# Small columns spread through DRAM instead of by TensorE, in a four-layer graph kernel whose instruction order is computed from assumed costs

**The chip, the cores and the metric.** One core of a Trainium2 chip. The time is the device time of one execution in microseconds (us), the median of the runs of a kernel.

## The reference, cut to what matters

The input is `x`, 128 graphs of 64 nodes with 512 features, and `adj`, a 64 x 64 matrix for each graph. Four layers follow, each of them `x = x + layer(relu(layernorm(x)))`. The change touches three of them:

```python
# layer 1
s = (x @ w) @ a                                   # one score for each node
A = tanh((s[:, :, None] + s[:, None, :]) / 8) * 8
A = exp(leaky_relu(A, 0.1)) * adj
A = A / sum(A, -1) * sum(adj, -1)                 # the normaliser, one number for each row
out = A @ x @ w
# layer 2
weight = adj * exp(query @ key.T)
out = (weight / sum(weight, -1)) @ value
# layer 3
e = leaky_relu(sj[:, None, :] + si[:, :, None] + ab, 0.2)
trans = adj * exp(e); trans = trans / sum(trans, -1)
H = sum over k = 0, 1, 2 of (trans^k @ x) @ Wk[k] + bk[k]
```

All is float32.

## The kernel before

Sixteen groups of 8 graphs (512 nodes, 4 tiles of 128 nodes, two graphs in a tile) go first through layers 0 and 1, then, in a second half, through layers 2 and 3. The large products are Strassen products, so TensorE does seven block products for eight.

A node's score is a column: one number on each partition. For `s[i] + s[j]` each partition also needs the 64 scores of its graph along its free dimension. The kernel before does this with TensorE: it multiplies the column into a diagonal and multiplies that by a block of ones.

```python
def bcast_sum(col, row, r, extra=None):
    dg, p, z = Buf("dg"), Buf("ps"), Buf("ee")
    dve(0.42, lambda: nc.vector.tensor_mul(dg.t, ident2[:, None, :].to_broadcast([P, T, C]),
                                           row()[:, :, None].to_broadcast([P, T, C])), r, [dg])
    pe(c_mm(256, 1), lambda: nc.tensor.matmul(p.t[:, :T * C], ones_bd, dg.t.rearrange("p t c -> p (t c)"),
                                              start=True, stop=True), [dg], [p])
    # ... (layer 3 adds a constant to col)
    dve(0.42, lambda: nc.vector.tensor_add(z.t, p.t[:, :T * C].rearrange("p (t c) -> p t c", t=T),
                                           col()[:, :, None].to_broadcast([P, T, C])), [p, *r], [z])
    return z
# layer 1, normaliser: column sums by ones_bd, twice, and a reciprocal of 256 columns
    pe(c_mm(256, 2), sums, [z, ad], [pd])
    dve(2.0, lambda: nc.vector.reciprocal(rn.t, half(0)), [pd], [rn])
# layer 2: sums of the weights by eight passes of one column
    pd, rd = col_sums(PT, PTk), Buf("col")
    # ... four products of 512 columns, each scaled by rd and added to x
# layer 3
    dot(lambda h=h: h.t, lambda s=s: c3_b[:, s, :], lambda t=t, s=s: ss.t[:, t, s:s + 1], ...)
    z = bcast_sum(lambda: ss.t[:, :, 1], lambda: ss.t[:, :, 0], ssk, extra=kap)
```

`pe(cost, fn, reads, writes)` and its likes (`dve`, `act`, `pool`, `dma`) do not emit an instruction. They put an operation into a graph, with an assumed cost and the current priority `G.prio`. At the end `Graph.run` plays the whole program with these costs. At each step it takes the operation that can start first and, among equals, the one of the lowest priority number, and it emits the instructions in that order. On the chip every engine then keeps to its list.

```python
LATENCY = {"PE": 0.30, "DVE": 0.12, "ACT": 0.12, "POOL": 0.15, "SP": 2.0}
# ... in run(), after an operation o has been placed at time t:
end = t + o.cost + self.LATENCY[o.eng]
for q in o.succ:
    q.ready = max(q.ready, end if q.eng != o.eng else t + o.cost)
# ... the priorities
STRETCH, PERIOD1, PERIOD2, LEAD = (1.65, 1.86, 2.69, 2.67), 80.0, 75.8, 1.5
for g in range(NG):
    G.prio = (g - LEAD) * PERIOD1
    # load of group g ...
    G.prio = g * PERIOD1        # then layers 0 and 1; inside a layer, step(us) adds us * STRETCH[layer]
```

Note the line with `q.ready`. A successor on another engine waits for the latency, a successor on the same engine does not. All transfers are issued by SP (the engine SyncE), so a transfer that reads what another transfer wrote is taken to be ready as soon as the first one has been issued.

## Time and profile before

| | before |
|---|---|
| time, median of 3 runs | 2470.34 us |
| span of the profile (of an execution of 2473.58 us) | 2471.6 us |
| TensorE busy / not busy | 2416.3 us / 55.3 us |
| mean granted TensorE clock | 0.99 |
| period of one group, first half / second half | 73.84 / 74.18 us |

A period is the time from a point of one group to the same point of the next; sixteen periods make a half. "Not busy" is the span less the busy time.

### The profile page before, as it was taken

Reading aid. Unit: us, or ns where it says so; the run is one execution under the profiler, and the core shown is the slowest. Engines: PE = TensorE matmul, PEld = TensorE weight load, DVE = VectorE, ACT = ScalarE, POOL = GpSimd, SP = SyncE. Lnnn points to the kernel's source line nnn. Section 1 sums busy time; section 2 is a strip of 40 time slices with the busy share of each in tenths; the row PEclk is TensorE's granted clock in tenths of the full one; section 3 lists DMA queues with packets and bytes.
Section 4 is the critical chain, followed back from the end, with each engine's and each line's share of the span. In section 5 each row is a group of like instructions: output and inputs, shape, how many; then the busy total and the mean of one; then the engine's idle time right before and its main releaser. Section 6 shows DMA issues by size and latency. Waiting matters only on the chain.

```text
span 2471.6 us, 32994 instructions
## 1 busy us (share of the span) xinstructions
PE 2416.3 (98%) x12058; PEld 1878.4 (76%) x12058; DVE 1808.8 (73%) x4128; ACT 1176.1 (48%) x1626; POOL 723.9 (29%) x842
## 2 busy tenths in 40 slices
PE   8999999999999999999989999999999999999998
PEld 4566767776677776677777888888888888888886
DVE  8678888888888888888875566665566665566663
ACT  4355554655554555454633445343445343445321
POOL 3223344333444333444221212221212221212220
PEclk9989999999999999999999999999999999999998
DMA  5242222222222222222431233212223222222211
GB/s 187 68 103 52 60 59 66 73 56 49 63 64 61 73 56 52 60 69 56 120 111 46 58 69 69 69 43 61 55 69 73 61 48 60 56 69 67 58 22 34
DMA packets 323698, 163.39 MB, mean 66 GB/s; under 512 B 278096, under 2 KB 278096, under 8 KB 323536
## 3 DMA queue, kind: packets, MB, share of 16 engines
q1 hardware_dynamic: 323536, 161.28, 26.3%
q8 instruction: 95, 1.56, 0.3%
q14 instruction: 67, 0.55, 0.1%
HBM read 59.52 MB, written 34.60 MB: 38 GB/s over the span
## 4 chain that ended last, share of the span: by engine, by line
PE 86%; DVE 9%; ACT 2%; DMA 1%; issue 1%; POOL 0%; DVEq 0%; ACTq 0%; POOLq 0%
PE ps L570 56%; PE ps L779 15%; PE ps L509 3%; PE ps L883 2%; PE ps L834 2%; PE ps L697 2%; DVE s_s_vu_tt L562 2%; PE ps L804 2%; DVE rT_a L562 1%; DVE u L588 1%; PE ps L607 1%; DVE ee L722 1%; PE ps L869 1%; DVE z_hT L590 1%; ACT rT_a L520 1%
## 5 line engine op out<-in xcount | busy, mean ns | idle before, releaser
L570 PE MATMUL ps<-wb_mem,rT_a 128*128 128x256 f32 x2056 | 480.7, 382 | 8.1 <-ACT rT_a L520 4.5
L492 POOL TENSOR_TENSOR rs<-ve,mhalf 128x1 f32<-128x1 f32 x320 | 202.2, 634 | 919.9 <-DVE ve L491 841.3
L570 PEld LDWEIGHTS ps<-wb_mem,rT_a 128*128 128x128 f32 x2056 | 389.5, 191 | 80.6 <-issue 13.8
L500 ACT ACTIVATE h<-x,nm,rs 128x512 f32<-128x512 f32 x256 | 208.0, 815 | 319.0 <-DVE nm L499 309.0
L570 PE MATMUL ps<-wb_mem,s_s_vu_tt 128*128 128x256 f32 x1152 | 274.3, 381 | 1.2 <-DVE x L737 0.9
L570 PE MATMUL ps<-wb_mem,tmp_mB_s 128*128 128x256 f32 x1152 | 263.1, 380 | 0.0
L570 PEld LDWEIGHTS ps<-wb_mem,s_s_vu_tt 128*128 128x128 f32 x1152 | 219.0, 191 | 48.3 <-issue 14.4
L570 PE MATMUL ps<-wb_mem,mT_a 128*128 128x256 f32 x1016 | 246.8, 382 | 5.7 <-DVE y_qT L600 5.0
L570 PE MATMUL ps<-wa_mem,mT_a 128*128 128x512 f32 x512 | 244.5, 602 | 2.8 <-ACT mT_a L511 1.5
L570 PEld LDWEIGHTS ps<-wb_mem,tmp_mB_s 128*128 128x128 f32 x1152 | 217.8, 190 | 37.0 <-issue 7.2
L570 PEld LDWEIGHTS ps<-wb_mem,mT_a 128*128 128x128 f32 x1016 | 188.7, 190 | 48.5 <-DVE y_qT L600 13.2
L538 ACT COPY u<-ps 128x256 f32<-128x256 f32 (+1 forms) x160 | 73.1, 457 | 277.7 <-PE ps L570 227.1
L570 PE MATMUL ps<-wa_mem,s_s_vu_tt 128*128 128x512 f32 x384 | 181.0, 595 | 1.5 <-DVE z_hT L590 1.0
L489 DVE BATCH_NORM_STATS2 st<-x 128x6 f32<-128x512 f32 x256 | 175.1, 684 | 3.6 <-DMA x<-xm 3.0
L570 PEld LDWEIGHTS ps<-wa_mem,mT_a 128*128 128x128 f32 x512 | 94.7, 192 | 95.5 <-issue 85.6
L896 POOL TENSOR_TENSOR u<-u,bk_b 128x256 f32<-128x256 f32 x96 | 79.1, 823 | 300.9 <-DVE u L542 177.8
L540 DVE TENSOR_TENSOR u<-ps,u 128x256 f32<-128x256 f32 (+1 forms) x160 | 84.5, 528 | 104.4 <-PE ps L570 44.3
L520 ACT COPY rT_a<-z_hT 128x1024 uint16<-128x1024 uint16 x128 | 145.9, 1160 | 15.5 <-DMA z_hT<-tmp_mB_s 15.4
L509 PEld LDWEIGHTS ps<-bd,h 128*128 128x128 f32 x1024 | 129.5, 195 | 24.1 <-issue 10.8
L518 ACT COPY o<-h 128x1024 uint16<-128x1024 uint16 x128 | 133.3, 1041 | 22.9 <-DVE o L358 21.3
L677 ACT ACTIVATE z_hT<-z_hT 128x512 f32<-128x512 f32 x128 | 80.5, 630 | 127.5 <-DVE z_hT L590 124.0
L666 POOL TENSOR_TENSOR x<-x,h 128x512 f32<-128x512 f32 x64 | 91.1, 1423 | 169.2 <-ACT h L500 168.9
(181 smaller groups left out, 4242.6 us busy)
## 6 DMA issues: line engine op xcount, KB each, us to landing
x<-in_x_dram SPq DMA_DIRECT2D x64, 256.0 KB, 2.7
xm<-x SPq DMA_DIRECT2D x64, 256.0 KB, 2.0
x<-xm SPq DMA_DIRECT2D x64, 256.0 KB, 2.8
out_dram<-x SPq DMA_DIRECT2D x64, 256.0 KB, 2.0
adj<-in_adj_dram SPq DMA_DIRECT2D x32, 256.0 KB, 2.9
wb_mem<-in_Wk_dram SPq DMA_DIRECT2D x6, 512.0 KB, 6.6
wa_mem<-in_W1T_dram SPq DMA_DIRECT2D x2, 1024.0 KB, 8.5
wb_mem<-in_W2T_dram SPq DMA_DIRECT2D x4, 512.0 KB, 6.2
```

Of the source, the lines that this page charges most:

```text
L489: dve(0.69, lambda i=i: nc.vector.bn_stats(st.t[:, i, :], src(i)), [r[i]], [(st, i)])
L492: pool(0.57, lambda: nc.gpsimd.tensor_tensor(rs.t, ve.t, mhalf, ALU.pow), [ve], [rs])
L500: act(0.82, lambda: nc.scalar.activation(h.t, xx.t, AF.Relu, bias=nm.t, scale=rs.t), [xx, nm, rs], [h])
L509: nc.tensor.matmul(quad(p)[:, c, :], h.t[:, c * P:(c + 1) * P], rhs(), start=True, stop=True)
L518: act(1.05, lambda: nc.scalar.copy(u16(planes.t).rearrange("p (q c) -> p q c", q=2), u16(src()).rearrange("p (c q) -> p q c", q=2)), ksrc, ...
L520: act(1.16, lambda: nc.scalar.copy(u16(dst()).rearrange("p c (k q) -> p c k q", q=2), u16(back()).rearrange("p (q c r) -> p c r q", q=2, c ...
L540: dve(c_v(n), lambda: nc.vector.tensor_add(at(1)(), p2.t[:, :n], at(0)()), [p2, (U, 0)], [(U, 1)])
L570: nc.tensor.matmul(p.t[:, :n], lhs()[:, c, :], rhs(c), start=first and c == 0, stop=c == kc - 1, skip_group_check=True)
L666: pool(1.3, lambda xx=xx, h=h: nc.gpsimd.tensor_add(xx.t, xx.t, h.t), [h, xx], [xx])
L677: act(0.63, lambda: nc.scalar.activation(z.t[:, cols], z.t[:, cols], AF.Relu), [(z, j)], [(z, j)])
L779: nc.tensor.matmul(pair(p.t)[:, o, :], a, b, start=first and o == 0 and c == 0, stop=c == 1, skip_group_check=True)
L896: pool(0.75, lambda: nc.gpsimd.tensor_add(U.t[:, iv], U.t[:, u[1]], add()), [u, ka], [v])
```

## The change

The intent is to take small work off TensorE, the bound engine, and to thin out the edges. It has five parts: (1) a column is stored to DRAM (`row`) and loaded back onto all 64 partitions of its graph (`rw`), for layer 1's and layer 3's scores and for layer 1's normaliser, which is now summed along the free dimension; (2) layer 2's `v` gets a column of ones, so its product brings the sums along; (3) layer 2's weight product moves to the start; (4) the loads of the setup and of W3 are placed anew; (5) the numbers of the priorities are new, with the preludes of layers 1 and 3 (the chain of small steps before the large products) drawn forward by 10.2 and 24.2 us.

```diff
+    def across(col, r):
+        b = Buf("rw")
+        d = dram.tile([P, T], F32, name=f"row{len(rows)}")
+        key = ("row", len(rows))
+        rows.append(d)
+        dma(4, lambda: nc.sync.dma_start(d, col()), r, [key])
+        def back():
+            for s in HALVES:
+                nc.sync.dma_start(b.t[s].rearrange("p c t -> p (c t)"),
+                                  d[s].rearrange("c t -> (c t)").partition_broadcast(C))
+        dma(128, back, [key], [b])
+        return b
     def bcast_sum(col, row, r, extra=None):
-        # diagonal product, matmul by ones_bd, sum out of PSUM
+        b, z = across(row, r), Buf("ee")
+        # ...
+        dve(0.42, lambda: nc.vector.tensor_add(z.t, by_node(b), col()[:, :, None].to_broadcast([P, T, C])), [b, *r], [z])
@@ layer 1, normaliser @@
-        pe(c_mm(256, 2), sums, [z, ad], [pd])
-        dve(2.0, lambda: nc.vector.reciprocal(rn.t, half(0)), [pd], [rn])
+        # num, den: two sums along the free dimension, then den = num / den (4 columns)
+        rn = across(lambda: den.t, [den])
@@ layer 2 @@
-        pd, rd = col_sums(PT, PTk), Buf("col")
+        # v is [P, 2, D + 1]; two products for each tile, of 257 and 256 columns; one reciprocal for each tile
@@ layer 3 @@
+        G.prio -= KNOBS[1]                      # layer 1 likewise with KNOBS[0]
@@ costs and priorities @@
-        return G.op("SP", kb / 190.0, fn, r, w)
+        return G.op("SP", kb / 350.0, fn, r, w)
-    STRETCH, PERIOD1, PERIOD2, LEAD = (1.65, 1.86, 2.69, 2.67), 80.0, 75.8, 1.5
+    STRETCH, PERIOD1, PERIOD2, LEAD = (1.72, 2.82, 2.69, 2.68), 81.0, 75.5, 0.88
+    KNOBS = (10.2, 24.2, 45.0, 88.7, 160.0, -976.9, -988.0, -973.4, -974.0, 5.0, -970.0, -939.5,)
# ... cut: setup_l2 at the start, W3's loads, rows for gamma and beta, the loop of layer 3's setup
```

More of the change, by code (lines that the diff above doesn't have):

```diff
@@ L181, in tile_adj_preln_d4 @@
         "u5": ([P, 3, D], 2), "u2": ([P, 3, D // 2], 1),
-        "bd": ([P, T, P], 4), "dg": ([P, T, C], 1), "ee": ([P, T, C], 2),
+        "bd": ([P, T, P], 4), "rw": ([P, C, T], 1), "ee": ([P, T, C], 2),
         "st": ([P, 2, 6], 6), "mv": ([P, 2], 10), "ve": ([P, 1], 10), "rs": ([P, 1], 10), "nm": ([P, 1], 10),
@@ L190, in tile_adj_preln_d4 @@
         ([("rT", [P, KH, P], 3)], [("a3", [P, 3 * KD, P], 2)]),
-        ([("s2", [P, 3, 4, P], 1), ("s1", [P, 3, 2, P], 2)], [("vu", [P, 2, D], 2), ("tt", [P, T, 2, P], 1)]),
+        ([("s2", [P, 3, 4, P], 1), ("s1", [P, 3, 2, P], 2)], [("vu", [P, 2, D + 1], 2), ("tt", [P, T, 2, P], 1)]),
         ([("y", [P, D], 2)], [("qT", [P, 2, 2 * P], 2)]),
@@ L264, in dma @@
     def dma(kb, fn, r, w):
-        return G.op("SP", kb / 190.0, fn, r, w)
+        return G.op("SP", kb / 350.0, fn, r, w)
     def quad(b):
         return b.t.rearrange("p (c k) -> p c k", c=4)
+    STRETCH, PERIOD1, PERIOD2, LEAD = (1.72, 2.82, 2.69, 2.68), 81.0, 75.5, 0.88
+    KNOBS = (10.2, 24.2, 45.0, 88.7, 160.0, -976.9, -988.0, -973.4, -974.0, 5.0, -970.0, -939.5,)
+    HEAD = KNOBS[5:]
     ident = const.tile([P, P], F32, name="ident")
     make_identity(nc, ident)
-    ident2 = const.tile([P, C], F32, name="ident2")
-    nc.vector.tensor_add(ident2, ident[:, :C], ident[:, C:])
     ones = const.tile([P, P], F32, name="ones")
     nc.vector.memset(ones, 1.0)
-    ones_bd = const.tile([P, P], F32, name="ones_bd")
-    nc.vector.memset(ones_bd, 0.0)
-    for s in HALVES:
-        nc.vector.memset(ones_bd[s, s], 1.0)
     mhalf = const.tile([P, 1], F32, name="mhalf")
@@ L313, in temp, with load_group @@
         return load_tmp("tmp", D, lambda t: t, src)
-    xt, adjs, xmid = {}, {}, {}
-    def load_group(g, src):
+    xt, adjs, xmid, rows = {}, {}, {}, []
+    def load_group(g, src, apart=0.0):
         b = Buf("adj")
@@ L323, in load_group @@
             at, key = src(g, t)
+            G.prio += apart
             dma(256, lambda xx=xx, at=at: nc.sync.dma_start(xx.t, at), key, [xx])
@@ L334, in tile_adj_preln_d4 @@
     G.prio = -1000.0
-    load_group(0, x_in)
+    bq_c = load_cols("bq_c", bq, KD)
+    load_group(0, x_in, HEAD[4])
+    G.prio = HEAD[5]
     load_w("w1", w1_sb, W1T)
     b1_b = [load_row(b1[i * D:(i + 1) * D]) for i in range(2)]
-    gb2 = const.tile([P, KH, 2], F32, name="gb2")
-    dma(8, lambda: nc.sync.dma_start(gb2[:, :, 0], gamma), [], ["gb2g"])
-    dma(8, lambda: nc.sync.dma_start(gb2[:, :, 1], beta), [], ["gb2b"])
+    G.prio = HEAD[6]
+    gb2 = const.tile([P, 2, KH], F32, name="gb2")
+    dma(8, lambda: nc.sync.dma_start(gb2[:, 0, :], gamma), [], ["gb2g"])
+    dma(8, lambda: nc.sync.dma_start(gb2[:, 1, :], beta), [], ["gb2b"])
     load_w("w2", w2_sb, W2T)
@@ L344, in tile_adj_preln_d4 @@
     load_w("w", w_sb, w)
-    bq_c = load_cols("bq_c", bq, KD)
     wa_b = Buf("row")
@@ L359, in dot, with combine @@
                                                          accum_out=acc()), r, [*w, j])
-    def combine(name, w_, x_, kc, n, eng):
+    def combine(name, w_, x_, kc, n, eng, olds=()):
         k2 = [w_[:, :kc, :], w_[:, kc:, :]]
@@ L369, in combine @@
         T1 = name + "T1"
-        G.op(eng, cost, lambda: sub(x_[:, 1], blk(1, 1), blk(0, 1)), [*low, *high], [(name, "x1")])
-        G.op(eng, cost, lambda: sub(blk(0, 1), blk(0, 1), blk(0, 0)), [*low, (name, "x1")], [T1])
+        G.op(eng, cost, lambda: sub(x_[:, 1], blk(1, 1), blk(0, 1)), [*low, *high], [(name, "x1"), *olds])
+        G.op(eng, cost, lambda: sub(blk(0, 1), blk(0, 1), blk(0, 0)), [*low, (name, "x1")], [T1, (name, "given")])
         G.op(eng, cost, lambda: sub(x_[:, 0], blk(1, 1), blk(0, 1)), [*high, T1], [(name, "x0")])
@@ L414, in setup_l0 @@
         gsc = const.tile([P, KH, 2], F32, name="gsc")
-        dve(0.2, lambda: nc.vector.tensor_scalar(gsc[:, :, 0], gb2[:, :, 0], 1.0 / DH, None, op0=ALU.mult), ["gb2g"], ["gsc0"])
-        dve(0.2, lambda: nc.vector.tensor_copy(gsc[:, :, 1], gb2[:, :, 1]), ["gb2b"], ["gsc1"])
+        dve(0.2, lambda: nc.vector.tensor_scalar(gsc[:, :, 0], gb2[:, 0, :], 1.0 / DH, None, op0=ALU.mult), ["gb2g"], ["gsc0"])
+        dve(0.2, lambda: nc.vector.tensor_copy(gsc[:, :, 1], gb2[:, 1, :]), ["gb2b"], ["gsc1"])
         def mm():
@@ L428, in setup_l0 @@
             dve(0.75, lambda c=c: nc.vector.scalar_tensor_tensor(
-                w2_sb[:, c, :], w2_sb[:, c, :], gb2[:, c, 0:1], pm.t, op0=ALU.mult, op1=ALU.subtract),
+                w2_sb[:, c, :], w2_sb[:, c, :], gb2[:, 0, c:c + 1], pm.t, op0=ALU.mult, op1=ALU.subtract),
                 [pm, "gb2g"], [("w2", c // 2)])
@@ L442, in setup_l1, with setup_l2 @@
         for c in range(KD):
-            dot(lambda c=c: w_sb[:, c, :], lambda: a_b.t, lambda c=c: wa.t[:, c:c + 1], [("w", c // 2), a_b], [(wa, c)])
+            dot(lambda c=c: w_sb[:, c, :], lambda: a_b.t, lambda c=c: wa.t[:, c:c + 1], [("w", c // 2), ("w", "given"), a_b], [(wa, c)])
         spread(lambda: wa.t, lambda: wa_b.t, [(wa, c) for c in range(KD)], wa_b)
-    def setup_l2():
+    def setup_l2(at):
         ps, pg = [Buf("ps") for _ in range(KD)], Buf("ps")
         for o in range(KD):
+            G.prio = at[o]
             q_, k_ = temp(Wq[o * P:(o + 1) * P, :]), temp(Wk[o * P:(o + 1) * P, :])
@@ L470, in setup_l3 @@
         ab_t = load_tmp("rs", 1, lambda t: t, ab.partition_broadcast(P))
+        av, cc = [temp(aw[s * D:(s + 1) * D].partition_broadcast(P)) for s in range(2)], [Buf("col"), Buf("col")]
         for s in range(2):
-            av, cc = temp(aw[s * D:(s + 1) * D].partition_broadcast(P)), Buf("col")
-            dot(lambda: bv_t.t, lambda av=av: av.t, lambda s=s: kk.t[:, s:s + 1], [bv_t, av], [(kk, s)])
-            for c in range(KD):
-                wv = temp(Wv3[c * P:(c + 1) * P, :])
-                dot(lambda wv=wv: wv.t, lambda av=av: av.t, lambda c=c, cc=cc: cc.t[:, c:c + 1], [wv, av], [(cc, c)])
-            spread(lambda cc=cc: cc.t, lambda s=s: c3_b[:, s, :], [(cc, c) for c in range(KD)], ("c3", s))
+            dot(lambda: bv_t.t, lambda s=s: av[s].t, lambda s=s: kk.t[:, s:s + 1], [bv_t, av[s]], [(kk, s)])
+        for c in range(KD):
+            wv = temp(Wv3[c * P:(c + 1) * P, :])
+            for s in range(2):
+                dot(lambda wv=wv: wv.t, lambda s=s: av[s].t, lambda c=c, s=s: cc[s].t[:, c:c + 1], [wv, av[s]], [(cc[s], c)])
+        for s in range(2):
+            spread(lambda s=s: cc[s].t, lambda s=s: c3_b[:, s, :], [(cc[s], c) for c in range(KD)], ("c3", s))
         dve(0.15, lambda: nc.vector.tensor_add(kap, kk.t[:, 0:1], kk.t[:, 1:2]), [(kk, 0), (kk, 1)], ["kap"])
@@ L518, in transposed @@
         act(1.05, lambda: nc.scalar.copy(u16(planes.t).rearrange("p (q c) -> p q c", q=2), u16(src()).rearrange("p (c q) -> p q c", q=2)), ksrc, [planes])
-        dma(200, lambda: nc.sync.dma_start_transpose(u16(back()).rearrange("p (b r) -> p b r", r=P), u16(planes.t)), [planes], kback)
+        dma(370, lambda: nc.sync.dma_start_transpose(u16(back()).rearrange("p (b r) -> p b r", r=P), u16(planes.t)), [planes], kback)
         act(1.16, lambda: nc.scalar.copy(u16(dst()).rearrange("p c (k q) -> p c k q", q=2), u16(back()).rearrange("p (q c r) -> p c r q", q=2, c=KD)), kback, kdst)
@@ L600, in biased, with by_node @@
         dve(c_v(D // 2, True), lambda: nc.vector.tensor_add(dst.t[:, cols], p.t[:, :D // 2], add()), [p, ka], [(dst, j)])
+    def across(col, r):
[6 more added lines that the diff above has]
+            for s in HALVES:
+                nc.sync.dma_start(b.t[s].rearrange("p c t -> p (c t)"), d[s].rearrange("c t -> (c t)").partition_broadcast(C))
+        dma(128, back, [key], [b])
+        return b
+    def by_node(b, s=slice(0, P)):
+        return b.t[s].rearrange("p c t -> p t c")
     def bcast_sum(col, row, r, extra=None):
-        dg, p, z = Buf("dg"), Buf("ps"), Buf("ee")
-        dve(0.42, lambda: nc.vector.tensor_mul(dg.t, ident2[:, None, :].to_broadcast([P, T, C]),
-                                               row()[:, :, None].to_broadcast([P, T, C])), r, [dg])
-        pe(c_mm(256, 1), lambda: nc.tensor.matmul(p.t[:, :T * C], ones_bd, dg.t.rearrange("p t c -> p (t c)"), start=True, stop=True), [dg], [p])
+        b, z = across(row, r), Buf("ee")
         if extra is not None:
@@ L611, in bcast_sum @@
             col, r = (lambda: ce.t), [ce]
-        dve(0.42, lambda: nc.vector.tensor_add(z.t, p.t[:, :T * C].rearrange("p (t c) -> p t c", t=T),
-                                               col()[:, :, None].to_broadcast([P, T, C])), [p, *r], [z])
+        dve(0.42, lambda: nc.vector.tensor_add(z.t, by_node(b), col()[:, :, None].to_broadcast([P, T, C])), [b, *r], [z])
         return z
@@ L620, in tok @@
         return slice(t * P, (t + 1) * P)
-    def col_sums(bd, r):
-        p = Buf("ps")
-        def mm():
-            for t in range(T):
-                nc.tensor.matmul(p.t[:, t:t + 1], bd.t[:, t, :], ones[:, 0:1], start=True, stop=True)
-        pe(c_mm(1, T), mm, r, [p])
-        return p
     def layer0(g):
@@ L704, in layer1 @@
         hs, sg = [], Buf("col")
+        G.prio -= KNOBS[0]
         for t in range(T):
@@ L712, in layer1 @@
         act(0.42, lambda: nc.scalar.activation(z.t, z.t, AF.Exp, scale=8.0), [z], [z])
-        PT, pd, rn = Buf("bd"), Buf("ps"), Buf("ee")
-        dve(0.42, lambda: nc.vector.tensor_mul(z.t, z.t, ad.t[:, 1]), [z, ad], [z])
-        def sums():
-            for i, m in enumerate((lambda: z.t, lambda: ad.t[:, 1])):
-                nc.tensor.matmul(pd.t[:, i * T * C:(i + 1) * T * C], ones_bd, m().rearrange("p t c -> p (t c)"), start=True, stop=True)
-        pe(c_mm(256, 2), sums, [z, ad], [pd])
-        half = lambda i: pd.t[:, i * T * C:(i + 1) * T * C].rearrange("p (t c) -> p t c", t=T)
-        dve(2.0, lambda: nc.vector.reciprocal(rn.t, half(0)), [pd], [rn])
-        dve(0.42, lambda: nc.vector.tensor_mul(rn.t, rn.t, half(1)), [pd, rn], [rn])
+        PT, zz, den, num = Buf("bd"), Buf("ee"), Buf("col"), Buf("col")
+        dve(0.42, lambda: nc.vector.tensor_reduce(num.t, ad.t[:, 0], AX.X, ALU.add), [ad], [num])
+        dve(0.42, lambda: nc.vector.tensor_mul(zz.t, z.t, ad.t[:, 0]), [z, ad], [zz])
+        dve(0.42, lambda: nc.vector.tensor_reduce(den.t, zz.t, AX.X, ALU.add), [zz], [den])
+        dve(0.16, lambda: nc.vector.reciprocal(den.t, den.t), [den], [den])
+        dve(0.16, lambda: nc.vector.tensor_mul(den.t, den.t, num.t), [den, num], [den])
+        rn = across(lambda: den.t, [den])
+        dve(0.42, lambda: nc.vector.tensor_mul(z.t, z.t, ad.t[:, 1]), [ad, zz], [z])
         for s in HALVES:
-            dve(0.42, lambda s=s: nc.vector.tensor_mul(PT.t[s, :, s], z.t[s], rn.t[s]), [z, rn], [(PT, s.start)])
+            dve(0.42, lambda s=s: nc.vector.tensor_mul(PT.t[s, :, s], z.t[s], by_node(rn, s)), [z, rn], [(PT, s.start)])
         PTk = [(PT, 0), (PT, C)]
+        G.prio += KNOBS[0]
         step(1.0)
@@ L814, in layer2 @@
         vb = [Buf("vu"), Buf("vu")]
+        for v_ in vb:
+            pool(0.2, lambda v_=v_: nc.gpsimd.memset(v_.t[:, :, D // 2:D // 2 + 1], 1.0), [], [(v_, 2)])
         def emit_v(i, j, p, u, v):
-            cols = slice(j * D // 2, (j + 1) * D // 2)
+            cols, at = slice(j * D // 2, (j + 1) * D // 2), slice(j * (D // 2 + 1), j * (D // 2 + 1) + D // 2)
             bias = bv_b[:, None, cols].to_broadcast([P, 2, D // 2])
@@ L823, in emit_v @@
                 add, ka = (lambda: pair(U.t[:, iv])), v
-            dve(c_v(D), lambda: nc.vector.tensor_add(vb[i].t[:, :, cols], pair(p.t), add()), [p, ka], [(vb[i], j)])
+            dve(c_v(D), lambda: nc.vector.tensor_add(vb[i].t[:, :, at], pair(p.t), add()), [p, ka], [(vb[i], j)])
         hv = {**hs, 3: hs[4], 4: hs[3], 5: hs[7], 7: hs[5]}
@@ L829, in layer2 @@
         PTk = [(PT, 0), (PT, C)]
-        pd, rd = col_sums(PT, PTk), Buf("col")
-        dve(0.18, lambda: nc.vector.reciprocal(rd.t, pd.t[:, :T]), [pd], [rd])
         for t in range(T):
-            xx, p = xt[g, t], Buf("ps")
-            pe(c_mm(512, 1), lambda p=p, t=t: nc.tensor.matmul(p.t, PT.t[:, t, :], vb[t // 2].t[:, t % 2, :], start=True, stop=True), [*PTk, (vb[t // 2], 0), (vb[t // 2], 1)], [p])
-            dve(0.75, lambda p=p, xx=xx, t=t: nc.vector.scalar_tensor_tensor(
-                xx.t, p.t, rd.t[:, t:t + 1], xx.t, op0=ALU.mult, op1=ALU.add), [p, rd, xx], [xx])
+            xx, ps, rd, v_ = xt[g, t], [Buf("ps"), Buf("ps")], Buf("ve"), vb[t // 2]
+            for j, (c0, c1) in enumerate(((0, D // 2 + 1), (D // 2 + 1, D + 1))):
+                pe(c_mm(256, 1), lambda p=ps[j], t=t, v_=v_, c0=c0, c1=c1: nc.tensor.matmul(
+                    p.t[:, :c1 - c0], PT.t[:, t, :], v_.t[:, t % 2, c0:c1], start=True, stop=True),
+                   [*PTk, (v_, j)] + ([(v_, 2)] if j == 0 else []), [ps[j]])
+            dve(0.16, lambda p=ps[0], rd=rd: nc.vector.reciprocal(rd.t, p.t[:, D // 2:D // 2 + 1]), [ps[0]], [rd])
+            for j in range(2):
+                cols = slice(j * D // 2, (j + 1) * D // 2)
+                dve(0.42, lambda p=ps[j], xx=xx, rd=rd, cols=cols: nc.vector.scalar_tensor_tensor(
+                    xx.t[:, cols], p.t[:, :D // 2], rd.t, xx.t[:, cols], op0=ALU.mult, op1=ALU.add), [ps[j], rd, xx], [xx])
             step(0.9)
@@ L871, in layer3 @@
         act(0.59, lambda: nc.scalar.copy(tt.t[:, :, 1, :], quad(p2)), [p2], [(tt, 1)])
+        G.prio += KNOBS[1]
         step(2.0)
@@ L915, in step @@
         G.prio += us * stretch[0]
-    STRETCH, PERIOD1, PERIOD2, LEAD = (1.65, 1.86, 2.69, 2.67), 80.0, 75.8, 1.5
     stretch = [STRETCH[0]]
+    setup_l2(HEAD[:4])
     G.prio = -900.0
@@ L931, in tile_adj_preln_d4 @@
         if g == 2:
-            G.prio = g * PERIOD1
-            setup_l2()
+            G.prio = KNOBS[4]
             setup_l3()
@@ L945, in tile_adj_preln_d4 @@
     dma(256, lambda: nc.sync.dma_start(bv_b, bv.partition_broadcast(P)), [], ["bv_b"])
-    olds2 = [k for n, kk in (("w2", KH), ("w", KD)) for k in (*wkeys(n, 0, kk), n + "T1", *[(n, f"x{i}") for i in range(3)])]
+    olds = lambda n, k: [*wkeys(n, 0, k), n + "T1", *[(n, f"x{i}") for i in range(3)]]
+    G.prio = NG * PERIOD1 + KNOBS[3]
     for k in range(3):
@@ L950, in tile_adj_preln_d4 @@
             i = k * KD + c
-            dma(512, lambda i=i, c=c, src=src: nc.sync.dma_start(w3_sb[:, i:i + 2, :], src[:, c:c + 2, :]), [], [("w3", i // 2), *olds2])
-    W3 = combine("w3", w3_sb, w3_x, 6, D // 2, "DVE")
+            dma(512, lambda i=i, c=c, src=src: nc.sync.dma_start(w3_sb[:, i:i + 2, :], src[:, c:c + 2, :]), [], [("w3", i // 2), *olds("w2", KH)])
+    W3 = combine("w3", w3_sb, w3_x, 6, D // 2, "DVE", [*olds("w2", KH), *olds("w", KD)])
     for g in range(NG):
@@ L955, in tile_adj_preln_d4 @@
         load_group(g, x_mid)
-        G.prio = NG * PERIOD1 + g * PERIOD2
+        G.prio = NG * PERIOD1 + g * PERIOD2 - (KNOBS[2] if g == NG - 1 else 0.0)
         for i, layer in ((2, layer2), (3, layer3)):
```

## The prediction

> **What bounds the kernel now.** I first read the page's totals and its 40 slices.
>
> ```profile
> PE 2416.3 (98%) x12058; PEld 1878.4 (76%) x12058; DVE 1808.8 (73%) x4128; ACT 1176.1 (48%) x1626; POOL 723.9 (29%) x842
> ...
> PE   8999999999999999999989999999999999999998
> ...
> PEclk9989999999999999999999999999999999999998
> ```
>
> TensorE is busy 98% of the span, and the chain that ended last puts 86% of the time on it. "Busy" could still hide slow matmuls, so I read the timeline. In the steady stretch every fp32 matmul is two passes, and eight passes of 256 columns start every 1.73 us (0.216 each), eight of 512 every 3.45. They run without a hole, so the rate is the engine's own. Next, the windows of one period in each half (two groups of layers 0+1, then two of layers 2+3; columns: window, its us, then busy PE, PEld, DVE, ACT, POOL, clock, DMA share, GB/s):
>
> ```profile
> 531.54:605.38 73.84, 73.37 (x310) 53.01 (x310) 62.42 (x146) 40.95 (x59) 28.29 (x32) 1.00 0.24 61
> 1605.07:1679.25 74.18, 74.18 (x439) 62.74 (x438) 47.72 (x108) 32.23 (x43) 17.36 (x20) 1.00 0.25 61
> ```
>
> The reader is to see that a period loses 0.47 us at most, and that VectorE has 11 us of room in the first half and 26 in the second. So time goes only with TensorE work, or at the edges. The edges are where the timeline shows TensorE idle (brackets: idle before, and what ended it):
>
> ```profile
> 11.43 6.49 PE L509 MATMUL ps<-bd,h 128*128 128x128 f32 x24 [3.69 <-ACT h L500]
> 147.85 3.78 PE L570 MATMUL ps<-wb_mem,rT_a 128*128 128x256 f32 x8 [4.46 <-ACT rT_a L520]
> 1289.08 3.78 PE L779 MATMUL ps<-z_hT,wa_mem 128*128 128x256 f32 x8 [6.52 <-ACT z_hT L520]
> 2419.34 1.11 PE L863 MATMUL ps<-ident,bd 128*128 128x128 f32 x4 [3.64 <-DVE bd L858]
> 2423.88 5.50 PE L883 MATMUL ps<-s_s_vu_tt,h 64*128 64x128 f32 x48 [0.68 <-ACT s_s_vu_tt L871]
> ```
>
> A hole costs twice: the 48 passes of the last line start to next in 5.43 us, and in 2.87 in the steady state; the eight passes after the 4.46 and 6.52 us holes take twice the usual 1.73. My ledger of edges: *start* (to 17.7 us, dense from there) 17.7 less 3.6 of useful work = 14; *60 to 175 us*, where the setup of layers 2 and 3 is mixed in, idle 9.3 (0.41+0.37+1.24+1.46+0.68+0.65+4.46) and a granted clock of 0.95, 0.84 and 0.93 in its 25 us windows from 100, some 5 more = 14; *changeover* (1280 to 1320) idle 11 and slow passes 4 = 15; *tail* (2412 to 2432) idle 7.8 (2.76+3.64+0.68+0.68) and slow passes 4 = 12, plus 4 us from the last matmul to the end. Together some 59 us.
>
> **What the Trainium skill says.** "TensorE: Matmul & The Clock Gate", LDWEIGHTS (loading the stationary operand): a load takes its columns / 1.2 ns, 107 for 128. The eight one-column passes of L628 below occupy 0.81 us, 0.101 each, so they cost their weight loads; this agrees. The same page, What's actually happening: an idle window of about 3.4 us puts the array at half clock, and a like busy one restores it; the doubled passes after the holes agree. "DMA: Bandwidth & Descriptors", Anatomy of one DMA: about 2.0 us fixed, mostly completion. The page's 256 KB transfers land in a median 2.0 to 2.8 us, and the smallest (0.5 to 4 KB) only ran in crowded stretches, 5.7 to 9.0, so no quiet small one is shown. "VectorE: DVE Perf Modes", First, the fixed hardware budget: a reciprocal repeats its divide eight times. Measured, 1.756 us on 256 columns against 0.42 for a multiply.
>
> **The change part by part.** The matmuls that go are visible in one period of each half:
>
> ```profile
> 584.32 0.59 PE L607 MATMUL ps<-dg,ones_bd 128*128 128x256 f32 x2
> 584.75 1.00 PE L650 MATMUL ps<-tmp_mB_s,bd 128*128 128x65 f32 x8
> ...
> 589.12 0.59 PE L719 MATMUL ps<-ee,ones_bd 128*128 128x256 f32 x2
> 589.55 0.59 PE L719 MATMUL ps<-adj,ones_bd 128*128 128x256 f32 x2
> 589.98 1.88 PE L570 MATMUL ps<-wa_mem,s_s_vu_tt 128*128 128x512 f32 x4
> ...
> 1649.76 0.95 PE L628 MATMUL ps<-ones,bd 128*128 128x1 f32 x8
> 1650.57 2.82 PE L834 MATMUL ps<-s_s_vu_tt,bd 128*128 128x512 f32 x6
> ```
>
> The second column includes the drain, so the cost is start to next start.
> Layer 1: the broadcast of scores 584.75 - 584.32 = 0.43, the two sums 589.98 - 589.12 = 0.86; together 1.29 per group.
> Layer 3: its broadcast 0.53 (1668.61 to 1669.14; two plain passes would be 0.43). Layer 2: column sums 0.81. Together 1.34.
> Layer 2's product becomes twice as many passes of 256 and 257 columns: 16 x 0.216 = 3.45 against 8 x 0.43 = 3.45, as 256-column passes hide their 0.19 us loads everywhere else; the extra column adds under 0.01 a group.
> All these lie on the bound engine: 16 x (1.29 + 1.34) = **42 us** gone.
>
> VectorE. Layer 1 loses the diagonal product 0.43, the reciprocal 1.76 and a multiply 0.42; it gains a multiply and two sums (3 x 0.42) and two small operations (0.34): about -1.0 net. Layer 3 loses 0.42. Layer 2 trades 4 x 0.75 + 0.18 for 8 x 0.42 + 4 x 0.18, +0.9. All inside VectorE's room: worth nothing. So are the 32 tiny GpSimd memsets.
>
> The trip through DRAM. Each spread is a store and a dependent pair of loads: by the medians above 2.0 + 2.7 plus issue, an estimated 5 us and more, where diagonal product, matmul and wait took 584.95 - 581.82 = 3.1 us. Layer 1 does two, layer 3 one; its chain grows perhaps 5 to 8 us and 3 us. No engine is occupied by it, and 48 round trips of 128 KB or so do not matter on a DMA system busy 26%. The change begins these preludes 10.2 and 24.2 us earlier in priority, which should cover it. Danger: SyncE's in-order queue stands waiting much of the time (649 us behind one ScalarE line), and four of the five h buffers are held longer.
>
> Setup, start. Layer 2's weight product (32 passes of 512 columns, 13.8 us, and 32 of one, 3.2) moves from 75 to 119 us to the very start, where TensorE waits 14 us for W1 and the first normalised tile. But Wq and Wk bring 2 MB: the DMA moved 225 to 410 GB/s there, so W1 can land some 3 us later than before, and the product starts on a cold clock. Four tmp buffers, one of which another setup holds, limit how much comes early. Gamma and beta get contiguous rows: beta's issue alone kept SyncE 4.52 us. Net estimate **-8**.
> *60 to 175 us*: the weight product, its five PSUM banks and buffers leave; layer 3's setup stays, with four Wv3 loads fewer. 14 to 5: **-9**.
> Changeover: W3 waits for W2 only, and is placed later, behind the first transposes. The 7.1 us of VectorE combining (four of 1.77 from 1286.93) that stood ahead of the second group's normalisation still must be done. 15 to 8: **-7**.
> Tail: the last group is drawn 45 us forward, so it shares TensorE with the group before it, instead of running its score chain with nothing beside it. 12 to 4: **-8**.
> Steady holes: 0.47 in most of 16 periods, half to go: **-3**; new waits on the trip in the transients: **+3**.
> Sum: -42 - 8 - 9 - 7 - 8 - 3 + 3 = -74, so 2470.3 - 74 = **2396 us**.
>
> **The rivals.** (a) *The trip becomes the wait.* For it: SyncE's blocking, the buffers, and a chain up to 8 us longer that must recur in every period. Against it: steady-state holes are 0.47 us now, and work of other groups is at hand. At 1 us of hole per layer 1 or 3 prelude, 32 us come back: 2428. (b) *Only the removed matmuls count*: the edges move rather than shrink, as filling needs the same loads and VectorE. For it: a dense start needs data that cannot come faster. Result 2470 - 42 = 2428, still just short of 2%. (c) *VectorE takes over the first half*: at 62.4 busy of 72.5 and falling by 1.0, no. (d) *All edges close*: 42 + some 50 gives 2378; 6 us before any data and 4 at the end remain anyway.
>
> **Range and chances.** 2% is at 2421. The 42 us are nearly certain, so slower by 2% needs a failure of the trip in all periods: 0.02. To pass 2% another 8 us must come from 59 us of edges and not be lost to (a): 0.84. The range runs from nearly all edges closed, 2370, to (a) or (b), 2428.
>
> **What would show it.** Right: no L607, L719 or L628 kind left, periods of about 72.4 and 72.9; the one-column and 512-column products of the setup within the first 25 us; less idle before the first product of the second layer-2 group; the tail's clock at 1.00. Wrong: holes before layer 1's or layer 3's left products ended by the DMA of the spread; periods that stay near 74; 257-column passes slower than 0.22 us; a first W1 product well after 22 us.

## More of the kernel before

The profile's span is some 2 us shorter than the timed run.

One line is wanted later for comparison, the first of the chain of waits that ended last, with each engine's share of the span:

```profile
PE 86%; DVE 9%; ACT 2%; DMA 1%; issue 1%; POOL 0%; DVEq 0%; ACTq 0%; POOLq 0%
```

Followed back from the end, the kernel before is one long row of TensorE work, and transfers are 1% of it.

## The result

The changed kernel is correct and takes 2661.3 us (2657.93 to 2667.43, 4 runs) against 2471.15 us (2470.01 to 2473.36, 4 runs) for the kernel before. The ratio is 1.077, with a 95% interval of 1.075 to 1.079. Here and below a ratio is the mean time of one kernel's fast runs over that of the other's fast runs of the same rounds, so it is not quite the ratio of the medians. The prediction was 2396 us, faster, with a range up to 2428. It is wrong in direction.

The page of the changed kernel: totals, the slices, and the first line of the chain that ended last.

```profile
PE 2426.4 (91%) x11930; PEld 1902.2 (72%) x11930; DVE 1817.7 (68%) x4252; ACT 1162.2 (44%) x1626; POOL 724.8 (27%) x874
...
PE   8999999999999999998888998889988889888897
...
PEclk9999999999999999999998999999999999999998
...
PE 29%; DVE 7%; DMA 7%; ACT 2%; issue 1%; POOL 0%; SPq 0%; DVEq 0%; ACTq 0%
```

The reader is to see two things. TensorE does 128 passes less (11930 against 12058), as the diff says, and is still busy 10 us longer; and it is not busy for 2658.2 - 2426.4 = 231.8 us, against 55.3 before. So of the 187 us between the spans, 176 are holes. The passes themselves are also slower: the granted clock is 0.964. The eights lie in the second half above all. The chain can be followed back only to 1424 us here, so its shares add up to 46% of the span and not to 99% as before; transfers are 7 of these 46, against 1 of 99.

The windows of one period in each half, taken between the same points as those of the prediction, with the same columns:

```profile
601.85:679.73 77.88, 74.31 (x304) 53.33 (x304) 62.07 (x148) 40.59 (x59) 27.57 (x32) 0.98 0.25 62
1942.87:2024.82 81.95, 74.75 (x437) 64.32 (x437) 48.65 (x115) 31.46 (x43) 17.54 (x22) 0.96 0.26 58
```

A period has become 4.0 us longer in the first half and 7.8 us in the second. Sixteen of each make 189 us, about all of the 187 us between the spans: the loss lies in every group, not at the edges. VectorE has as much room as before (62 of 78, 49 of 82), so it is not the bound.

What ended the holes: the waits of TensorE, then of VectorE, then of the DMA queue (engine, line, releaser; us in total, times, longest).

```profile
PE ps L881 <- DVE bd L876: 120.2, 16, 10.8
PE ps L515 <- DVE bd L734: 37.6, 16, 3.3
PE ps L576 <- DVE u L548: 26.9, 17, 2.8
```

```profile
DVE ee L632 <- DMA rw<-row: 166.4, 32, 10.7
...
DVE bd L734 <- DMA rw<-row: 43.6, 21, 3.2
```

```profile
SPq L618 <- DMA row<-ss: 104.2, 16, 8.0
...
SPq L618 <- DMA row<-col: 47.1, 32, 4.7
```

L881 are layer 3's transposes, L515 in this place layer 1's product by the normalised matrix. TensorE waits for VectorE in both, but VectorE was itself waiting: L632 is the sum that reads the spread column (in layers 1 and 3), and it stands 166 us for the load `rw<-row`; L734, the product by layer 1's spread normaliser, stands another 44. The load in turn stands 104 us for layer 3's store `row<-ss`, 6.5 us each time, and 47 for layer 1's `row<-col`, 1.5 each. A wait that names an engine must be followed one step further when that engine was waiting too.

The timeline of one group's layer 3 (start, us, engine, line, what; brackets: idle before and what ended it):

```profile
2010.73 0.58 SPq L614 DMA_DIRECT2D row<-ss  x1
...
2017.44 1.10 SPq L618 DMA_DIRECT2D rw<-row  x2
...
2021.03 0.60 DVE L632 TENSOR_TENSOR ee<-rw,col 128x256 f32<-128x256 f32 x1 [6.88 <-DMA rw<-row]
...
2024.82 1.11 PE L881 MATMUL ps<-ident,bd 128*128 128x128 f32 x4 [6.52 <-DVE bd L876]
...
2025.72 3.23 PE L789 MATMUL ps<-wa_mem,z_hT 128*128 128x256 f32 x8
```

From the issue of the store to the sum are 10.3 us, of which 6.7 are the store alone. VectorE does nothing at all for 6.88 us of it, and TensorE runs dry for 6.52. After the hole the eight passes of L789 need 3.07 us from start to the next start, instead of 1.73: the hole is paid again in slow passes.

In layer 1 a trip is shorter: 4.6 us from 670.58 to 675.19 for the scores, 4.8 from 679.63 to 684.45 for the normaliser, about what the prediction estimated:

```profile
670.58 0.33 SPq L614 DMA_DIRECT2D row<-col  x1
...
672.00 1.09 SPq L618 DMA_DIRECT2D rw<-row  x2
...
675.19 0.61 DVE L632 TENSOR_TENSOR ee<-rw,col 128x256 f32<-128x256 f32 x1 [2.17 <-DMA rw<-row]
...
679.63 0.58 SPq L614 DMA_DIRECT2D row<-col  x1
...
684.45 1.24 DVE L734 TENSOR_TENSOR bd<-ee,rw 64x256 f32<-64x256 f32 x2 [2.54 <-DMA rw<-row]
685.75 2.68 PE L515 MATMUL ps<-bd,h 128*128 128x128 f32 x16 [2.31 <-DVE bd L734]
```

The difference between the two stores is in the list of transfers (issues, KB each, median us from issue to landing):

```profile
row<-col SPq DMA_DIRECT2D x32, 2.0 KB, 2.0
...
row<-ss SPq DMA_DIRECT2D x16, 2.0 KB, 6.9
```

Both carry 2 KB. Layer 1's column `[128, 4]` lies in 128 pieces of 16 bytes. Layer 3's is `ss[:, :, 1]` of a tile `[128, 4, 2]`: every second number, 512 pieces of 4 bytes.

My theory after this was: (A) the 4-byte store is the larger part; (B) the dependent load behind every store is a second part, since the order-maker counts no latency for it; and the rival (C): the new priorities do not suit this program, so holes would come even without a trip. (C) gained weight when I looked at what `run` returns, the total that the order-maker computes for its own order: 2452.8 for the kernel before, which the chip does in 2471, and 2401.8 for the changed one, which takes 2661. For the new kernel the model from which the order is built is off by 260 us.

### The profile page after: what moved, and what is told of

Same layout as the page of the kernel before. It is cut to its first block, busy times and chain, and to the rows that moved or that the text cites. A ratio compares the mean times of both kernels' runs of the same rounds, so it can differ in the third digit from the quotient of the medians.

```text
span 2658.2 us, 32983 instructions
## 1 busy us (share of the span) xinstructions
PE 2426.4 (91%) x11930; PEld 1902.2 (72%) x11930; DVE 1817.7 (68%) x4252; ACT 1162.2 (44%) x1626; POOL 724.8 (27%) x874
## 2 busy tenths in 40 slices
DMA packets 342068, 168.75 MB, mean 63 GB/s; under 512 B 290832, under 2 KB 296976, under 8 KB 341904
## 5 line engine op out<-in xcount | busy, mean ns | idle before, releaser
L515 PEld LDWEIGHTS ps<-bd,h 128*128 128x128 f32 x1024 | 147.4, 215 | 67.5 <-DVE bd L734 44.4
L515 PE MATMUL ps<-bd,h 128*128 128x128 f32 x1024 | 152.1, 302 | 41.4 <-DVE bd L734 37.6
L604 POOL TENSOR_TENSOR u<-u,row_sh_q 128x256 f32<-128x256 f32 x96 | 70.2, 739 | 401.5 <-DVE u L546 376.4
L915 POOL TENSOR_TENSOR u<-u,bk_b 128x256 f32<-128x256 f32 x96 | 84.9, 886 | 279.1 <-DVE u L548 173.6
```

What stands on the lines that cost most here:

```text
L515: nc.tensor.matmul(quad(p)[:, c, :], h.t[:, c * P:(c + 1) * P], rhs(), start=True, stop=True)
L604: pool(0.75, lambda: nc.gpsimd.tensor_add(U.t[:, iv], U.t[:, iu], row()[:, cols]), [u, krow], [v])
L915: pool(0.75, lambda: nc.gpsimd.tensor_add(U.t[:, iv], U.t[:, u[1]], add()), [u, ka], [v])
```

## The experiments

Each kernel ran in three timed rounds and once with a profile, beside the kernel before (2471.8 to 2473.4 us, median of 7 runs in each of the three batches). "The changed kernel" is the one of the result.

**Layer 3's store in 128 pieces of 16 bytes.** The order-maker sees no difference, so every engine keeps the changed kernel's order.

```diff
-        "col": ([P, T], 24), "ss": ([P, T, 2], 2),
+        "col": ([P, T], 24), "ss": ([P, 2, T], 2),
-     ... lambda t=t, s=s: ss.t[:, t, s:s + 1], ...
+     ... lambda t=t, s=s: ss.t[:, s, t:t + 1], ...
-        z = bcast_sum(lambda: ss.t[:, :, 1], lambda: ss.t[:, :, 0], ssk, extra=kap)
+        z = bcast_sum(lambda: ss.t[:, 1], lambda: ss.t[:, 0], ssk, extra=kap)
```

> Layer 3's scores are kept as two contiguous columns, so that the store to DRAM leaves as 128 pieces of 16 bytes instead of 512 of 4 bytes; every engine's order of instructions is the same as in the changed kernel. Theory A (the 4-byte store is the largest part of the loss): the store lands in 2.0 us, as layer 1's does, instead of 6.9; the hole before the transposes of layer 3 falls from about 6.4 to 1.5 us per group, and the slow passes behind it (1.6 us a group) go too: 16 x (4.9 + 1.6) = 104 us, so 2661 becomes 2550 to 2580. Rival B (the round trip as such, or SyncE's queue, sets the wait, and the form of the store does not matter): the load still comes late, 2640 or more.

Measured 2554.15 us, ratio 1.033 (1.032 to 1.035): 107 us less than the changed kernel. From its list of transfers, and from its waits of TensorE:

```profile
row<-ss SPq DMA_DIRECT2D x16, 2.0 KB, 1.4
```

```profile
PE ps L881 <- DVE bd L876: 30.0, 16, 4.9
```

The store lands in 1.4 us instead of 6.9, and layer 3's holes shrink from 120 to 30 us. The number of DMA packets in the profile falls by 6144 (342068 to 335924), which is 16 x (512 - 128). Theory A is shown, and it is more than half of the loss. 81 us above the kernel before remain.

**Layer 3's scores, or layer 1's scores and normaliser, by TensorE again, the rest as changed.** Two kernels; each puts the old diagonal product, matmul and sum back for one layer.

```diff
-        z = bcast_sum(lambda: ss.t[:, :, 1], lambda: ss.t[:, :, 0], ssk, extra=kap)
+        z = bcast_mm(lambda: ss.t[:, :, 1], lambda: ss.t[:, :, 0], ssk, extra=kap)   # the old bcast_sum
```

> Only layer 3's scores go back to the diagonal product and the matmul; layer 1 keeps its two trips, layer 2 its column of ones, the loads their new places. Trips theory (A or B): the second half's period falls from 81.8 us to about 73.4 (74.2 less the 0.81 of the column sums), 16 x 8.4 = 134 us, so about 2525 to 2540. Rival C (the column of ones with its 257-column passes, or the new priorities, slow the second half): the period stays above 78 and the time above 2600.

Measured 2624.17 us, ratio 1.061 (1.059 to 1.064). Theory A had asked for a gain like that of the contiguous store; it came to 37 us. The second half's period stays at 81.9 us. This is what rival C had forecast (above 78 and above 2600).

> Only layer 1 goes back to matmuls and the wide reciprocal; layer 3 keeps its trip with the 4-byte store. Trips theory: the first half's period falls from 77.8 to about 73.8 us, 16 x 4 = 64 us, so about 2597; the second half keeps its 81.8. Rival C (the new priorities and load places slow the first half): the period stays near 77 and the time above 2640.

Measured 2638.4 us, ratio 1.067 (1.066 to 1.069): 23 us less than the changed kernel, about a third of the gain that was expected. The first half's period is about 77.0 us (154.09 for two groups), again near what rival C had forecast. Both are misses of the trips theory. The likely common cause is that adding operations makes the order anew, with the same priorities; the fits below bear on it.

**No trips at all.** Both of the above; what stays of the change is the column of ones, the places of setup and W3, and the numbers of the priorities.

> Both layers by matmul again; what is left of the change is layer 2's column of ones, the new places of the loads and the new priorities. If the parts add: 2661 - 134 - 64 = 2463. If the edges also shrink as my prediction's ledger says (13 us of column sums and about 30 of edges off the 2471 of before): 2425 to 2435. If the new priorities are themselves harmful: above 2475.

Measured 2600.59 us, ratio 1.053 (1.051 to 1.055). By its parts this kernel should have beaten the kernel before: it has 13 us less TensorE work and no trip. It is 127 us slower, as the third branch of the expectation said. The order-maker itself computes 2509.7 us for it, so it knows that this order is worse than that of the changed kernel. One period, and the holes in the second half, again in layer 3 at the transposes:

```profile
1807.74:1889.66 81.92, 77.63 (x438) 66.95 (x439) 48.60 (x116) 32.28 (x43) 15.82 (x22) 0.94 0.23 55
```

```profile
1884.40 0.59 PE L646 MATMUL ps<-dg,ones_bd 128*128 128x256 f32 x2
1884.83 1.89 PE L811 MATMUL ps<-wa_mem,z_hT 128*128 128x256 f32 x8
1889.66 1.11 PE L903 MATMUL ps<-ident,bd 128*128 128x128 f32 x4 [2.94 <-DVE bd L898]
...
1894.20 5.36 PE L924 MATMUL ps<-s_s_vu_tt,h 64*128 64x128 f32 x48 [0.68 <-ACT s_s_vu_tt L911]
```

Between the broadcast (L646) and the transposes (L903) TensorE has eight passes, 1.73 us of work, for a chain on VectorE and ScalarE that takes 4.8. In the kernel before, 24 passes of other groups (1669.14 to 1674.33, 5.2 us) stand in this place, and there is no hole. After the hole the 48 passes of L924 take 5.30 us to the next start, against 2.87 in the steady state (granted clock 0.50 to 0.54 in these passes). So holes of this kind need no DMA: the rival C has a share. This is a property of the order, not of an instruction.

**The load does not wait for its store (wrong result).** The contiguous store of the first experiment; the load reads a constant row that was written once. Every engine keeps the changed kernel's order; store, load and bytes stay.

```diff
+    row0 = dram.tile([P, T], F32, name="row_fixed"); nc.sync.dma_start(row0, ones[:, :T])
-                nc.sync.dma_start(..., d[s].rearrange("c t -> (c t)").partition_broadcast(C))
+                nc.sync.dma_start(..., row0[s].rearrange("c t -> (c t)").partition_broadcast(C))
```

> Wrong result on purpose. As e1_ss_contiguous, same order of instructions on every engine, but the load that spreads the row over partitions reads a row of ones written once at the start, so it no longer waits for its store. Theory F (the kernel's own order-maker gives a dependent DMA on the same queue no latency after the DMA it depends on, so it puts the readers on VectorE some 2 us too early, 48 times, and the holes are these 2 us): the holes before layer 1's left product, layer 1's 512-wide products and layer 3's transposes nearly vanish, and the time goes from 2554 to 2420 to 2460, near the 2402 that the order-maker itself computes. Rival G (the rest of the loss is the new priorities, the strided reads of 0.61 us or the queue's traffic): 2520 or more.

Measured 2479.99 us, ratio 1.004 (1.002 to 1.005): 74 us less than with the dependence. Shown is that the wait of a load for its own store costs 74 us; that it hurts because the order-maker leaves it out is read from the code and not tested by this run. The size fell short: the time lies above the expected 2420 to 2460, and 78 us above the order-maker's 2402. Against the kernel before, TensorE is now busy 29 us less (2386.9) and not busy 38 us more (93.0); 23.0 us are layer 1's holes at L515 and 10.3 layer 3's at L881. So even with both faults of the trip removed nothing of the predicted gain appears. I did not separate this remainder further; candidates are the time of the loads themselves, the 1.1 us that SP needs to issue the pair, the slower sums (below) and the slow passes.

**The same with the 4-byte store, which nothing now waits for (wrong result).**

> Wrong result on purpose. The same step from the changed kernel itself: layer 3's store is still 512 pieces of 4 bytes, but nothing waits for it. If the 4-byte store hurts only because its landing is waited for, this equals u1_load_not_dependent within 10 us. If it also clogs the queue for the loads and transposes behind it, it is 30 us or more slower than that.

Measured 2573.25 us, ratio 1.041 (1.040 to 1.043), 93 us above the run before this one. Nobody reads that store, and still it costs. The transfers from 1300 to 2470 us, first with the 4-byte store, then with the 16-byte one:

```profile
rw<-row_fixed SPq DMA_DIRECT2D x30, 64.0 KB, 6.8
...
row<-ss SPq DMA_DIRECT2D x15, 2.0 KB, 7.3
```

```profile
rw<-row_fixed SPq DMA_DIRECT2D x32, 64.0 KB, 2.6
...
row<-ss SPq DMA_DIRECT2D x16, 2.0 KB, 1.6
```

The loads that come behind the store land 4.2 us later, though they depend on nothing that it writes. So the 512 pieces hold up what stands behind them as well; taking the wait away would not have healed it. How the loss is shared out depends on which fault is removed first: in the other order, the wait is worth 88 us (2661.3 - 2573.25) and the form 93, the sum of 181 being the same.

**The latency counted, the priorities as changed.** One line of the order-maker, on the kernel with the contiguous store: a transfer that depends on a transfer waits 2 us too.

```diff
-                q.ready = max(q.ready, end if q.eng != o.eng else t + o.cost)
+                q.ready = max(q.ready, end if q.eng != o.eng or o.eng == "SP" else t + o.cost)
```

> As e1_ss_contiguous, but the order-maker now gives every DMA its 2 us also before a dependent DMA of the same queue (one line); all priorities as in the change. If a truthful order alone mends it: 2440 to 2480. If the priorities were fitted to the untruthful one, so that the new order is merely another one with its own holes (a replay of this order with in-order engines gives 2594 to 2630): 2590 to 2680.

Measured 2722.54 us, ratio 1.102 (1.100 to 1.103), 168 us worse than the same kernel with the untrue latency. This is the second branch of the expectation, and 42 us worse than its range. A truer model alone does not help; that the priorities had been fitted to the other one is the likely reason, not one that this run shows.

**The column of ones alone, on the kernel before.**

```diff
-        pd, rd = col_sums(PT, PTk), Buf("col")
+        # ones in v, two products of 257 and 256 columns, a reciprocal for each tile, as in the change
```

> The kernel before with layer 2's column of ones alone, priorities and loads as before. By parts: 16 x 0.81 = 13 us less, 2458. If every edit makes the order anew and the old priorities only fit the old graph (the replay gives 2546 to 2572): 2560 to 2610, slower than before although TensorE has less to do.

Measured 2559.64 us, ratio 1.036 (1.034 to 1.038). By its parts it should have taken 2472 - 13 = 2459; it came out at the lower end of the second branch. The first half's period stays at 73.8 us, the second half's becomes about 80, with holes of 4.33 us at layer 3's transposes. The order-maker's own total is 2528.1 us, 75 above its 2452.8 for the kernel before. Priorities that served that kernel do not serve one with a changed layer 2. This widens C: an edit of the operations or their costs makes the order anew, and with the old numbers it is measured together with the damage to the order.

**The priorities fitted again.** To tell the parts from the order, I searched the 19 numbers of STRETCH, the periods, LEAD and KNOBS at random for three kernels. Each candidate order was played with every engine keeping to its list, the latency counted for every transfer, and passes slow after a hole. The search only picks an order, and the times below are the chip's. All three use the line of the honest latency.

> As e4_no_trips (matmuls in layers 1 and 3, column of ones in layer 2, new places of the loads), with the truthful order-maker and the 19 priority numbers searched anew; a replay of the order with in-order engines, the order-maker's costs, the slow clock after holes and 2 us for every DMA gives 2427. Theory (most of what e4 and o1 lost was the order, not the operations): below before, 2420 to 2460. Rival (the column of ones with its pairs of PSUM banks, or the new load places, cost by themselves): above 2500.

The kernel without trips: 2441.59 us, ratio 0.988 (0.986 to 0.989). It differs from the 2600.59 us of the same kernel above only in that line and the numbers, and gains 159 us. Its periods:

```profile
711.49:784.75 73.26, 73.26 (x311) 53.15 (x310) 61.18 (x146) 40.99 (x59) 27.63 (x32) 1.00 0.27 62
1720.02:1794.59 74.57, 73.22 (x439) 63.50 (x438) 47.79 (x116) 32.10 (x43) 16.95 (x22) 1.00 0.25 58
```

TensorE is busy again for all but at most 1.35 us of a period, at full clock. This version is faster than both kernels, by 1.2% (its interval excludes 1) and 8.3% (2661.3 less 2441.59, over 2661.3).

> As e1_ss_contiguous (three trips through DRAM per group of layers, contiguous store), truthful order-maker, measured costs for the trip and the strided reads, and the priority numbers searched anew; the replay gives 2467. If the trips can be hidden once the order knows of them, it equals or beats n1_no_trips_refitted, as 27 us of TensorE work are gone. If their latency still costs more than those matmuls: slower than n1, 2460 to 2510.

The kernel with trips, a contiguous store and measured costs for the trip: 2485.5 us, ratio 1.005 (1.004 to 1.007). Fitted again, the changed kernel gains 69 us over its contiguous version, but stays 44 us behind the one without trips, though it has less to do on TensorE.

> As n1_no_trips_refitted but with layer 2's column sums and 512-wide product of the kernel before: only the new places of the loads and a refitted, truthful order are left of the change. The replay gives 2436, 9 us more than n1 (the column of ones saves 13 us of TensorE). If the gain of n1 comes from loads and order alone, this is as fast as n1: 2425 to 2465.

The first of the three without the column of ones: 2455.09 us, ratio 0.993 (0.992 to 0.995). The column of ones is worth 2455.09 - 2441.59 = 13.5 us. The new places of setup and W3, with their own fit, are worth 2472.31 - 2455.09 = 17 us together; the kernel before was not fitted anew, so how much of that is the fit is open. These three compare the best orders that I found, not the best there are; a longer search could move each by some us, the 13.5 too. The replays had given 2427, 2467 and 2436: 15 to 19 us under the chip each time.

## Why the prediction was wrong

**What TensorE no longer does: right as work, wrong as time.** The passes are gone, and the column of ones brings 13.5 us where 16 x 0.81 = 13 were predicted (so close a match is partly luck, since each of the two kernels has its own fit). The product of 257 and 256 columns is as quick as hoped: in the kernel without trips, newly fitted, fourteen of its passes in a row (1767.86 to 1770.90) take 3.04 us, 0.217 each. The step that went on from there, "these lie on the bound engine: 42 us gone", takes for granted that the rest of the order stays tight. It did not.

**The step that failed.** It is this one: "No engine is occupied by it ... The change begins these preludes 10.2 and 24.2 us earlier in priority, which should cover it." Rival (a), the trip as the wait, was named, with the right sign in the profile (holes before the left products, ended by the spread's transfer), but sized at 1 us of hole for each prelude, 32 us. Measured are 157.8 us at L881 and L515, 4.9 for each of the 32 preludes, and slower passes behind them. A slower kernel had been given a chance of 0.02. In place of the failed step the runs show two causes, and a third is inferred:

1. *The form of layer 3's store, 107 us.* I had costed a store by its kilobytes, at about 2 us. The store of 512 pieces of 4 bytes lands in 6.9, and also delays what stands behind it. The Trainium skill says this: "DMA: Bandwidth & Descriptors", Rules for kernel authors, on a strided last dimension: "Lowers to one descriptor per element. Rearrange so the last dim is contiguous instead". This agrees, by the 6144 packets and by 6.9 us against 1.4 in the same place of the same order. The access `ss[:, :, 1]` was in the diff; I looked up what a transfer costs, not what this access makes of it.
2. *The dependent load, 74 us.* A trip is two landings in a row, and the order-maker counts none between them. So the consumer on VectorE was listed too early. VectorE keeps to its list and, at the sum L632, stood 166.4 us in the changed kernel, 77.6 with the contiguous store and 36.0 without the dependence; TensorE stood behind it. "No engine is occupied" was true of work, but SyncE stood 151 us behind the stores (104.2 + 47.1), and an engine that must wait in its list is as good as occupied.
3. *Numbers fitted to that model (inferred).* I took the new priorities for an improvement because the preludes were drawn forward. That they had been fitted to a model with this gap is an inference from the order-maker's totals: 2401.8 us for exactly this program, 2509.7 after putting the matmuls back. The trace of the kernel before could not show it, but the line with `q.ready` was in the code before me. The kernel without trips (2600.59 before the new fit, 2441.59 after) shows what the numbers alone can do.

By subtraction: 2661.3 - 107 - 74 = 2480, and from there to the predicted 2396 are another 84 us, whose cause stays open.

**Slow passes.** The prediction said that a hole costs twice, and used that only at the edges. Compare busy times: the newly fitted kernel without trips, whose mean clock is 0.998, is busy 2386.3 us with 16 x (1.29 + 0.53) = 29 us of matmuls that the changed kernel doesn't have. At that rate the changed kernel would be busy about 2357; it is busy 2426.4. So some 69 us (an estimate from these busy times) are passes at the lower clock. A part of it is measured directly: the kernel with the contiguous store, whose load does not wait, runs the same passes in the same order and is busy 2386.9 us. Of the 178 us between its span and the changed kernel's, 139 are holes and 39.5 are slower passes.

**VectorE.** Right that it does not become the bound. Missed: the sum that reads `rw` takes 0.61 us and not 0.42. From the groups of VectorE, before and after (count | busy us, mean ns | idle before):

```profile
L612 DVE TENSOR_TENSOR ee<-ps,col 128x256 f32<-128x256 f32 x32 | 13.5, 422 | 9.2 <-PE ps L607 9.2
```

```profile
L632 DVE TENSOR_TENSOR ee<-rw,col 128x256 f32<-128x256 f32 x32 | 19.4, 607 | 166.4 <-DMA rw<-row 166.4
```

`rw` holds the four tiles of a node side by side and is read with a step of 16 bytes. "SBUF — State Buffer", Specifications (TRN2), gives lines of 16 bytes that need two hits each for full bandwidth; that fits the 0.185 us more. But this pair mixes two changes, since the old sum read its operand from PSUM. Layer 1's product by the normaliser settles it: the same shape, no PSUM on either side, and only the second operand's step is new.

```profile
L725 DVE TENSOR_TENSOR bd<-ee,ee 64x256 f32<-64x256 f32 x32 | 13.4, 420 | 0.8
```

```profile
L734 DVE TENSOR_TENSOR bd<-ee,rw 64x256 f32<-64x256 f32 x32 | 19.4, 605 | 44.0 <-DMA rw<-row 43.6
```

The step costs 0.185 us here as well.

**Start, changeover and tail: 32 us predicted.** At the start the change does bring group 2's first product 17 us forward (102.0 instead of 119.4 us), as much as the predicted -8 and -9 together. That is partly luck, for the weight product ran at 43 to 65 us, not within the first 25, probably since a block of Wk needed a buffer that layer 0's setup still held (its load is issued at 39.34, right after that setup's last reader starts at 38.30). And group 3 starts at 200.1 instead of 187.0: the gain is lost by then. At the changeover the hole of 6.52 us is gone, as hoped: between 1283 and 1345 us the longest is 2.16. But a new one of 8.98 us stands before the first transposes of layer 3, and the tail has one of 9.86 us there, both behind the trip. Whether these gains are real is not shown; the 17 us of the version without trips and ones would allow it. None reached the end of this kernel.

**Small readings of the prediction that need a correction.** The 2.0 us of fixed time that it takes from "DMA: Bandwidth & Descriptors" stand there for the path through GpSimd, while these transfers are issued by SyncE; stores of 2 KB in 16-byte pieces landed in 1.4 to 2.0. It took 0.101 us for each one-column pass as agreeing with weight loads of 107 ns, while its own trace gives a load 0.19 us: the spacing fits, the duration does not. And of the 256 KB transfers that it put at 2.0 to 2.8 us, those of `adj` land in 2.9.

## What to carry to other kernels

A trip through DRAM costs two landings in a row, and its form counts more than its bytes: make the stored column contiguous on each partition, put both landings into whatever model places the instructions, and ask which in-order engine will stand at the far end. Where a kernel's order is searched against a cost model, an edit can be judged only after the search has been done again, with the edit's measured costs: the column of ones cost 2559.64 - 2471.77 = 88 us with the old numbers and gained 13.5 with new ones. Compare the model's own total with the chip first; a gap that grows with the change (20 us before, 260 after) tells that the model has lost touch.

## What the Trainium skill lacked or had wrong

- "DMA: Bandwidth & Descriptors" has the rule on strided dimensions but no time for so small a case: 512 pieces of 4 bytes land in 6.9 us, 128 pieces of 16 bytes in 1.4 to 2.0, the bytes being the same 2 KB.
- The same page does not tell what such a store costs the transfers behind it: loads of 64 KB that do not depend on it land in 6.8 us instead of 2.6, and a kernel in which nothing waits for the store still lost 93 us.
- "TensorE: Matmul & The Clock Gate" speaks of an idle window of about 3.4 us. Here passes were slow after less: a hole of 2.94 us was followed by 48 passes in 5.30 us instead of 2.87 (with two more of 0.68 between), and two holes of 1.25 and 2.31 us within 8 us by eight passes that took 2.81 us to the next start instead of 1.73. The granted clock was 0.50 to 0.54 in the first, 0.61 in the second.
- "SBUF — State Buffer" has no time for a stepped read: on VectorE the same product of 256 columns took 605 ns with one operand read in steps of 16 bytes, against 420 without steps.
- No page treats an order that is fixed when the kernel is built from assumed costs. What such an order can cost is shown by the kernel without trips: 2600.59 us with the changed kernel's numbers, 2441.59 with a new fit.
